# Thirteen expert jobs get their transposed tokens from VectorE and a DRAM exchange instead of from TensorE

## The chip, the cores and the metric

The kernel runs on one core of one Trainium2 chip. The metric is the time of the whole kernel on the device, in microseconds (us), as the median of several runs. The profile is that of one further execution.

## The reference, cut to what matters

The block takes 16 sequences of 256 tokens with 256 channels each: a normalisation with a shift, attention with 16 heads of width 64, a residual, and then a mixture of 8 experts. Every expert takes the 512 tokens that score highest for it (4096 tokens divided by 8), and adds its result to them, weighted by the gate:

```
gate = softmax(tok @ Wgate.T)
vals, idx = top_k(gate.T, 512)                  # for each expert
g = ln(tok[idx], mlp_g, mlp_b)
y = gelu(einsum('ked,ehd->keh', g, fc1s) + b1s) # 256 -> 1024
y = einsum('keh,edh->ked', y, fc2s) + b2s       # 1024 -> 256
tok = tok.at[idx].add(y * w)
```

All arithmetic of the large products is in float32.

## The kernel before

**Two parts.** The attention of all 16 sequences is laid out as a list of steps with written places (the long table `PLACES`); the steps are issued in that order. After it comes the loop over expert jobs, which the change touches. A job is one expert with one half of its tokens: there are two rounds of eight jobs. Jobs 0 to 7 take 256 tokens for each expert, chosen from the first 15 sequences; jobs 8 to 15 take 256 more for each, chosen from everything that is left. Jobs 0 and 1 are prepared inside the list of steps, and job 0's first matmuls too.

**One job.** `Job.load` (lines 1178 to 1186) brings the two weight matrices, 1 MB each, and the bias, on SP's DMA queue. `gives` and `onehot` (VectorE) make a table that says which token stands at which of the 256 places. `list_matmul` (line 1224, TensorE, 30 or 32 small matmuls) and `take` (lines 1233 and 1235, VectorE) turn it into two index columns and two weights. `gather` (line 1240) is two indirect DMAs from GpSimd (POOL) that fetch 128 normalised tokens of 1 KB each from `xn_dram` into `xg`. `transposes` (line 1249) turns the 256 tokens by 256 channels with four TensorE matmuls against the identity into PSUM tile `px`; `evict` (line 1256) copies it on ScalarE into `xT`, two instructions with the normalisation's gain and bias. Then come eight `up` steps (line 1268), each with a `gelu` (line 1275, ScalarE) after it, and eight `down` steps (line 1284), four for each half of the tokens. `finish` (line 1295, VectorE) weighs one half, and `scatter` (line 1301, POOL, an indirect DMA that adds) writes it to the output. The profile counts each float32 matmul of the source twice: an `up` or `down` step is four records, a job 64.

**The order of the work.** The loop runs k from 1 to 15. While job k computes, job k+1 (`new`) gets its list, its tokens and its transposes, and the one-hot table of job k+2 (`far`) is made. An iteration has 16 slots, one for each `up` or `down` step, and every engine receives its instructions in the order of the slots:

```
LIST_AT, TURN_AT, LATE_AT = 5, 14, 7
if new and s == (LATE_AT if late else LIST_AT):   # list_matmul, take, gather
if new and s == TURN_AT:                          # transposes, evict
```

Slots are an order of issue, not times: an engine goes ahead as far as its own data lets it, and all engines take their instructions strictly in this order. `lay_out(far)` starts one slot after `LIST_AT` and gives VectorE one piece (the table's head, then two or three one-hots) in each slot, through the end of the iteration and into the next one. At the end of iteration k, `far.load()` puts the weights of job k+2 on SP's queue; they go into the buffers of job k and so wait for its last `down`.

Iteration 7 is special (`late`): its `new`, job 8, is the first of the second round, so its whole one-hot table is made in slots 0 to 5 of that iteration and its list at slot 7. In iterations 1 to 6 the generator `second_routing` runs as well: at every fifth slot a small TensorE matmul (`count_three`, line 1049) and a group of VectorE instructions (`choose_bits`, `candidates`, `compare_three`, lines 1034 to 1064) search the second round's thresholds bit by bit.

**The exchange in the attention.** A way of transposing without TensorE is in use there already: VectorE turns blocks of 32 by 32 (lines 749 and 832, `STREAM_TRANSPOSE`), one DMA writes the turned blocks to a DRAM tile (lines 756 and 840), and four DMAs, one for each group of 32 partitions, read them back so that the blocks stand in exchanged places (lines 764 and 854).

Of the kernel before, what the change touches and what calls it, by code (L numbers as in the profile page):

```python
# [9 lines left out]
F32 = mybir.dt.float32  # L10
I32 = mybir.dt.int32
BF16 = mybir.dt.bfloat16
AF = mybir.ActivationFunctionType
# [5 lines left out]
P = 128  # L19
# [8 lines left out]
DC = D // P  # L28
# [3 lines left out]
KL = KC // 2  # L32
CAPL = CAP // 2
NV = 5
SQ = 32
QB = P // SQ
# [3 lines left out]
LN1_G, LN1_B, B_ADA, MLP_G, MLP_B = 0, 2, 4, 6, 8  # L40
# [4 lines left out]
class Plan:  # L45
# [7 lines left out]
    def step(self, place, engine, took, run, needs=(), makes=(), tiles=(), mode=0, lag=0.1):  # L53
        k = len(self.steps)
        self.steps.append((place, engine, took, run, needs, tiles, mode, lag))
        for m in makes:
            self.makers.setdefault(m, []).append(k)
# [7 lines left out]
def kernel(  # L65
# [14 lines left out]
    nc = tc.nc  # L80

    const = ctx.enter_context(tc.tile_pool(name="const", bufs=1))
    dram = ctx.enter_context(tc.tile_pool(name="dram", bufs=1, space=DRAM))
# [6 lines left out]
    vec = const.tile([P, NVEC], F32, name="vec")  # L90
# [432 lines left out]
    if True:  # L523
        attw = ctx.enter_context(tc.tile_pool(name="attw", bufs=1))
        seq = ctx.enter_context(tc.tile_pool(name="seq", bufs=2))
        work = ctx.enter_context(tc.tile_pool(name="work", bufs=2))
# [22 lines left out]
        class Shift:  # L549
            def __init__(self):  # L550
                self.pa = {}
# [75 lines left out]
        class First:  # L627
# [22 lines left out]
            def evict(self):  # L650
                b = self.b
                hTs[b] = seq.tile([P, DC, N], F32, tag="hT", name=f"hT{b}")
                for c in range(DC):
                    nc.scalar.activation(
                        hTs[b][:, c, :], self.pt[:, c, :], AF.Identity,
                        bias=bias1[:, c, b : b + 1],
                        scale=vec[:, LN1_G + c : LN1_G + c + 1],
                    )
# [12 lines left out]
        class Group:  # L671
# [74 lines left out]
            def turn(self, kb):  # L746
                if self.t == 0:
                    kb.append(work.tile([P, QB, TB, HP // 2, SQ], F32, tag="pb", bufs=3, name="kb"))
                nc.vector.transpose(
                    kb[0][:, :, self.t],  # L750
                    self.qk.rearrange("p (h q d) -> p q h d", q=QB, d=SQ),
                )

            def away(self, kb):
                self.blocks = dram.tile([QB, SQ, QB, N], F32, tag="blocks", bufs=4, name="kblocks")
                nc.sync.dma_start(
                    self.blocks.rearrange("k d q n -> (k d) (q n)"),
                    kb[0].rearrange("p q t h m -> p (q t h m)"),
                )

            def back(self):
                kT = self.keys()[:, self.g - 2].rearrange("p k t h m -> p k (t h m)")
                for q in range(QB):
                    nc.sync.dma_start(
                        kT[bass.ts(q, SQ)], self.blocks[:, :, q].rearrange("k d n -> d k n")
                    )

            def affine(self):
                kT = self.keys()[:, self.g - 2].rearrange("p k t h m -> p (k t h m)")
                nc.scalar.activation(  # L770
                    kT, kT, AF.Identity,
                    bias=vec[:, KN_B : KN_B + 1], scale=vec[:, KN_G : KN_G + 1],
                )
# [398 lines left out]
        class Job:  # L1172
            def __init__(self, e, routing, tiles):
                self.e, self.routing, self.tiles = e, routing, tiles
                self.oh = None

            def load(self):


                e = self.e  # L1180
                self.w2 = seq.tile([P, FC, D], F32, tag="oT", name="w2")
                nc.sync.dma_start(self.w2, fc2T[e].rearrange("(f p) d -> p f d", p=P))
                self.w1 = seq.tile([P, DC, DD], F32, tag="v", bufs=2, name="w1")
                nc.sync.dma_start(self.w1, fc1T[e].rearrange("(c p) f -> p c f", p=P))
                self.b2 = moe.tile([P, D], F32, tag="b2", bufs=2, name="b2")
                nc.sync.dma_start(self.b2, b2s[:, bass.ts(e, D)].to_broadcast([P, D]))
# [66 lines left out]
            def evict(self):  # L1253
                self.xT = seq.tile([P, DC, CAPL], F32, tag="hT", name="xT")
                for c in range(DC):
                    nc.scalar.activation(
                        self.xT[:, c, :], self.px[:, c, :], AF.Identity,
                        bias=vec[:, MLP_B + c : MLP_B + c + 1],
                        scale=vec[:, MLP_G + c : MLP_G + c + 1],
                    )  # L1260
                self.hid = seq.tile([P, FC, CAPL], F32, tag="qT", name="hid")
                self.y = work.tile([P, KL, D], F32, tag="pr", bufs=PRB, name="y")
                self.ph, self.py = {}, {}

            def up(self, f):
                self.ph[f] = ps.tile([P, CAPL], F32, tag="sc", bufs=4, name="ph")
                for c in range(DC):
                    nc.tensor.matmul(  # L1268
                        self.ph[f], self.w1[:, c, bass.ts(f, P)], self.xT[:, c, :],
                        start=(c == 0), stop=(c == DC - 1),  # L1270
                    )

            def gelu(self, f):
                k = B1 + self.e * FC + f
                nc.scalar.activation(  # L1275
                    self.hid[:, f, :], self.ph[f], AF.Gelu_apprx_tanh,
                    bias=vec[:, k : k + 1], scale=1.0,
                )

            def down(self, i, a=0, b=FC):  # L1280
# [51 lines left out]
        for b in range(B):  # L1332
# [16 lines left out]
            for (g, t), p in GROUP.items():  # L1349
                p += base  # L1350
                a = Group(b, g, t)
                n = (b, g, t)
# [23 lines left out]
            for d in range(HP // 2):  # L1376
                a = Quad(b, d)
                p = base + d * QUAD
                g = d // 2
                n = (b, d)  # L1380
                po = ("po", 0) + n
                for i in range(2):
                    q = p + 3 * i
                    m = n + (i,)
                    sums, pb, prT, blocks = ("sums",) + m, ("pb",) + m, ("prT",) + m, ("blocks",) + m
# [20 lines left out]
            for t in range(TB):  # L1406
                a = Tail(b, t)
                p = base + TAIL[t]
                n = (b, t)
# [55 lines left out]
        for n in range(2):  # L1465
            a = jobs[n]
            k = top + 10 + 20 * n
# [4 lines left out]
            for i in range(6):  # L1472
                name, took, by = {"D": ("DVE", 0.81, nc.vector), "P": ("POOL", 1.4, nc.gpsimd), "A": ("ACT", 3.5, nc.scalar)}[who[i]]
# [13 lines left out]
        k = top + 30  # L1487
# [9 lines left out]
        for k in plan.order(PLACES):  # L1497
            plan.steps[k][3]()

        LIST_AT, TURN_AT, LATE_AT = 5, 14, 7  # L1500
        SLOTS = 2 * FC

        def second_routing():
# [9 lines left out]
        def lay_out(job):  # L1513

            job.gives()
            for a in list(range(0, 18, 2)) + list(range(18, NT, 3)):
                yield
                job.onehot(a, a + (2 if a < 18 else 3))
# [5 lines left out]
        for k in range(1, len(jobs)):  # L1524
            a = jobs[k]
            new = jobs[k + 1] if k + 1 < len(jobs) else None
            far = jobs[k + 2] if k + 2 < len(jobs) else None
            late = k == last + 1
            for s in range(SLOTS):
                for step in next(rest, ()):  # L1530
                    step()
                if late and s == 0:
                    new.gives()
                if late and s < 6:
                    new.onehot(6 * s, 6 * s + 6)
                if new and s == (LATE_AT if late else LIST_AT):
                    for _ in () if late else parts:
                        pass
                    new.list_matmul(0, NT)
                    new.take()  # L1540
                    new.gather()
                    if k == 1:
                        jobs[0].scatter(by_end[1])
                if new and s == TURN_AT:
                    new.transposes()
                    new.evict()
                if not late and s < LIST_AT:
                    next(parts, None)
                if far and k != last and s > LIST_AT:
                    if s == LIST_AT + 1:  # L1550
                        parts = lay_out(far)
                    next(parts)
                if s < FC:
                    a.up(s)
                    a.gelu(s)
                    if s == FC - 1:
                        a.weigh()
                else:
                    i, q = divmod(s - FC, 4)
                    a.down(i, 2 * q, 2 * q + 2)  # L1560
                    if q == 3:
                        a.finish(i)
                        a.scatter(i)
            if far:
                far.load()
# [50 lines left out]
```

## Time and profile before

| | us |
|---|---|
| Runs shown | 1104.45, 1104.83, 1106.43 |
| Median | 1104.83 |
| The profiled execution, its time | 1106.04 |
| The profiled execution, its span (first to last instruction) | 1104.2 |

| Engine | busy us | share of the span |
|---|---|---|
| TensorE matmul (PE) | 1070.6 | 97% |
| VectorE (DVE) | 778.9 | 71% |
| GpSimd (POOL) | 616.2 | 56% |
| ScalarE (ACT) | 596.1 | 54% |

The granted clock of TensorE is 0.99 over the span. The expert loop begins at 865.6 us (first `up` of job 1) and its last matmul ends at about 1094.8 us. `SPq` names the instructions in SP's queue, almost all of them issues of DMAs. `px<-ident,xg` reads: written is `px`, read are `ident` and `xg`. `x4` means four instructions merged into one row. An entry in square brackets at the end of a row is the time for which the engine was idle before it, and what it waited for.

### The profile page before, as it was taken

Reading aid. Unit: us, or ns where it says so; the run is one execution under the profiler, and the core shown is the slowest. Engines: PE = TensorE matmul, PEld = TensorE weight load, DVE = VectorE, ACT = ScalarE, POOL = GpSimd, SP = SyncE. Lnnn points to the kernel's source line nnn. Section 1 sums busy time; section 2 is a strip of 40 time slices with the busy share of each in tenths; the row PEclk is TensorE's granted clock in tenths of the full one; section 3 lists DMA queues with packets and bytes.
Section 4 is the critical chain, followed back from the end, with each engine's and each line's share of the span. In section 5 each row is a group of like instructions: output and inputs, shape, how many; then the busy total and the mean of one; then the engine's idle time right before and its main releaser. Section 6 shows DMA issues by size and latency. Waiting matters only on the chain. (4 is left out here: it accounts for less than half of the span.)

```text
span 1104.2 us, 18872 instructions
## 1 busy us (share of the span) xinstructions
PE 1070.6 (97%) x5835; PEld 714.8 (65%) x5835; DVE 778.9 (71%) x2201; ACT 596.1 (54%) x1656; POOL 616.2 (56%) x997
## 2 busy tenths in 40 slices
PE   7999999999999999999899999999988999999996
PEld 4555656566565655656465655656767888888885
DVE  6657888777778777786678787676568488654540
ACT  2768666565766566566557667576522333322331
POOL 3766776776676665675657666565411233333332
PEclk9999999999999999999999999999999999999998
DMA  6013998785888787796787778895130456555661
GB/s 211 1 39 123 277 259 237 230 255 166 248 260 227 226 246 234 201 260 211 211 251 227 228 224 240 243 256 179 63 102 20 113 189 200 170 162 175 196 201 19
DMA packets 147539, 209.20 MB, mean 189 GB/s; under 512 B 15088, under 2 KB 122864, under 8 KB 147440
## 3 DMA queue, kind: packets, MB, share of 16 engines
q1 hardware_dynamic: 139520, 197.71, 60.0%
q0 software_dynamic: 6144, 8.39, 4.1%
q10 hardware_dynamic: 1776, 1.90, 0.5%
q8 instruction: 47, 0.77, 0.3%
q14 instruction: 52, 0.43, 0.1%
HBM read 121.96 MB, written 85.98 MB: 188 GB/s over the span
## 5 line engine op out<-in xcount | busy, mean ns | idle before, releaser
L683 PE MATMUL pm<-wq,hT 128*128 128x512 f32 x768 | 360.4, 605 | 5.0 <-DVE qk L716 2.8
L822 POOL TENSOR_SCALAR pr<-pr,sums 128x256 f32<-128x256 f32 x512 | 237.1, 481 | 112.2 <-DVE sums L818 92.9
L811 ACT ACTIVATE pr<-sc,nmax 128x256 f32<-128x256 f32 x512 | 238.0, 480 | 97.5 <-DVE nmax L802 80.3
L683 PEld LDWEIGHTS pm<-wq,hT 128*128 128x128 f32 x768 | 137.3, 192 | 146.1 <-issue 131.1
L103 POOL TENSOR_TENSOR ss<-ss,neghalf 128x8 f32<-128x8 f32 x128 | 210.5, 1645 | 10.6
L802 DVE TENSOR_REDUCE nmax<-sc 128x2 f32<-128x512 f32 x256 | 165.3, 676 | 16.9 <-PE sc L794 16.3
L832 DVE STREAM_TRANSPOSE pb<-pr 128x512 f32<-128x512 f32 x224 | 149.9, 690 | 18.5 <-POOL pr L822 13.6
L794 PE MATMUL sc<-kT,qT 64*128 64x256 f32 x1024 | 135.4, 397 | 0.0
L881 PE MATMUL po<-prT,v 128*64 128x256 f32 x1024 | 127.6, 388 | 1.1 <-DVE gates L950 1.1
L700 DVE TENSOR_REDUCE ss<-sq 128x8 f32<-128x512 f32 x128 | 86.0, 672 | 47.3 <-ACT sq L696 46.8
L794 PEld LDWEIGHTS sc<-kT,qT 64*128 64x128 f32 x1024 | 92.8, 188 | 40.8 <-issue 25.4
L696 ACT ACTIVATE sq<-pm 128x512 f32<-128x512 f32 x128 | 76.9, 603 | 77.3 <-PE pm L683 75.9
L1301 POOL DMA_INDIRECT out<-y,idx x32 | 51.2, 1601 | 119.8 <-DVE y L1295 66.9
L1268 PE MATMUL ph<-xT,w 128*128 128x256 f32 x512 | 117.6, 383 | 0.0
L907 PE MATMUL pw<-wo,oT 128*128 128x256 f32 x512 | 116.6, 381 | 0.3 <-DVE qk L716 0.3
L1284 PE MATMUL py<-w,hid 128*128 128x256 f32 x512 | 116.3, 380 | 0.0
L716 DVE TENSOR_TENSOR qk<-pm,ss 128x512 f32<-128x512 f32 x128 | 87.0, 681 | 36.9 <-POOL ss L103 35.9
L907 PEld LDWEIGHTS pw<-wo,oT 128*128 128x128 f32 x512 | 96.0, 190 | 23.2 <-issue 9.4
L811 ACT ACTIVATION_READ_ACCUMULATOR pr<-sc,nmax 128x1 f32 x512 | 107.6, 210 | 0.0
L881 PEld LDWEIGHTS po<-prT,v 128*64 128x64 f32 x1024 | 67.1, 137 | 61.5 <-issue 21.1
L1275 ACT ACTIVATE hid<-ph,vec 128x256 f32<-128x256 f32 x128 | 60.4, 474 | 84.2 <-PE ph L1268 76.3
L1284 PEld LDWEIGHTS py<-w,hid 128*128 128x128 f32 x512 | 95.6, 190 | 12.8
(140 smaller groups left out, 1132.6 us busy)
## 6 DMA issues: line engine op xcount, KB each, us to landing
blocks<-pb SPq DMA_DIRECT2D x112, 512.0 KB
prT<-blocks SPq DMA_DIRECT2D x448, 128.0 KB
w<-in_fc2T SPq DMA_DIRECT2D x16, 1024.0 KB
w<-in_fc1T SPq DMA_DIRECT2D x16, 1024.0 KB
kblocks<-kb SPq DMA_DIRECT2D x28, 512.0 KB
kT<-kblocks SPq DMA_DIRECT2D x112, 128.0 KB
out<-tok SPq DMA_DIRECT2D x32, 128.0 KB
xn_dram<-tn SPq DMA_DIRECT2D x32, 128.0 KB
```

What stands on the lines that cost most here:

```text
L103: nc.gpsimd.tensor_tensor(dst, src, neghalf[:, : src.shape[1]], ALU.pow)
L683: nc.tensor.matmul(self.pm, hTs[self.b][:, c, bass.ts(self.t, P)], wq[:, c, bass.ts(self.g, GW)], start=(c == 0), stop=(c == DC - 1),)
L716: engine.tensor_tensor(self.qk.rearrange("p (h d) -> p h d", d=HD), src.rearrange("p (h d) -> p h d", d=HD), self.ss[:, 1, :].unsqueeze(2) ...
L794: nc.tensor.matmul(self.sc[i, j][:, t, :], qTs[self.b][rows, hp, bass.ts(t, P)], keys[rows, hp] if direct else keys[rows, hp // 4, hp % 4] ...
L802: nc.vector.tensor_reduce(self.nmax[i, j], self.sc[i, j], AX.X, ALU.max, negate=True)
L811: nc.scalar.activation(self.pr[i, j][:, t, :], self.sc[i, j][:, t, :], AF.Exp, bias=self.nmax[i, j][:, t : t + 1], scale=1.0, accum_out=se ...
L822: nc.gpsimd.tensor_scalar(self.pr[i, j][:, t, :], self.pr[i, j][:, t, :], self.sums[i][:, 1, j, t : t + 1], 1.0, ALU.mult, ALU.mult,)
L832: nc.vector.transpose(self.pb[i][:, :, :, j].rearrange("p k c t n -> p t k c n"), self.pr[i, j].rearrange("p t (k c m) -> p t k c m", c=TB ...
L881: nc.tensor.matmul(self.po[j * HD : (j + 1) * HD, i, :], vs[self.b][:, c, bass.ts(4 * self.d + 2 * i + j, HD)], prT[:, j, c] if self.b in ...
L907: nc.tensor.matmul(self.pw, oTs[self.b][:, hp // 2, self.t, hp % 2, :], wo[:, hp, :], start=(hp == 0), stop=(hp == HP - 1),)
L1268: nc.tensor.matmul(self.ph[f], self.w1[:, c, bass.ts(f, P)], self.xT[:, c, :], start=(c == 0), stop=(c == DC - 1),)
L1284: nc.tensor.matmul(self.py[i], self.hid[:, f, bass.ts(i, P)], self.w2[:, f, :], start=(f == 0), stop=(f == FC - 1),)
```

## The change: what it does

For every `new` that is not `late`, which by the loop's bounds are jobs 2 to 7 and 9 to 15, thirteen in all, the four TensorE transposes and the eviction from PSUM are replaced by steps in four slots:

- slot 8, `turn`: two VectorE transposes of 32 by 32 blocks, each of 128 by 256 elements, from `xg` into a new tile `xb` (it uses buffers of the attention's `prT`);
- slot 9, `away`: one DMA on SP's queue, 256 KB, `xb` to the DRAM tile `xblocks`;
- slot 12, `back`: four DMAs on SP's queue, 64 KB each, from `xblocks` into `xT`; they wait for `away`'s landing;
- slot 15, `affine`: two ScalarE instructions of 128 by 256 that apply gain and bias to `xT` in place.

The tokens of `xT` then stand in another order (block of 32 first, half second). `up` reads its moving operand in pieces of 64 columns, and `gelu` writes its result back in the old order, in pieces of 32 columns; the rest of the job is as before. Jobs 0, 1 and 8 keep the old way.

The list step (`list_matmul`, `take`, `gather`) goes from slot 5 to slot 1, and with it the beginning of `lay_out(far)` from slot 6 to slot 2. In the first iteration the scatter of job 0's second half, which stands in the same step, moves along.

```
+            def turn(self):
+                self.xb = work.tile([P, QB, DC, KL, SQ], F32, tag="prT", bufs=4, name="xb")
+                for i in range(KL):
+                    nc.vector.transpose(
+                        self.xb[:, :, :, i].rearrange("p q c m -> p c q m"),
+                        self.xg[:, i].rearrange("p (c q d) -> p c q d", c=DC, d=SQ),
+                    )
+
+            def away(self):
+                self.blocks = dram.tile([QB, SQ, QB, P], F32, tag="xblocks", bufs=2, name="xblocks")
+                nc.sync.dma_start(
+                    self.blocks.rearrange("k d q n -> (k d) (q n)"),
+                    self.xb.rearrange("p q c i m -> p (q c i m)"),
+                )
+
+            def back(self):
+                self.xT = seq.tile([P, QB, DC, KL, SQ], F32, tag="hT", name="xT")
+                xT = self.xT.rearrange("p k c i m -> p k (c i m)")
+                for q in range(QB):
+                    nc.sync.dma_start(
+                        xT[bass.ts(q, SQ)], self.blocks[:, :, q].rearrange("k d n -> d k n")
+                    )
+
+            def affine(self):
+                for c in range(DC):
+                    xT = self.xT[:, :, c].rearrange("p k i m -> p k (i m)")
+                    nc.scalar.activation(
+                        xT, xT, AF.Identity,
+                        bias=vec[:, MLP_B + c : MLP_B + c + 1],
+                        scale=vec[:, MLP_G + c : MLP_G + c + 1],
+                    )
+                self.outputs()
...
-                        self.ph[f], self.w1[:, c, bass.ts(f, P)], self.xT[:, c, :],
+                        self.ph[f], self.w1[:, c, bass.ts(f, P)],
+                        self.xT[:, :, c].rearrange("p k i m -> p k (i m)") if self.exchanged else self.xT[:, c, :],
...
+                dst, src = self.hid[:, f, :], self.ph[f]
+                if self.exchanged:
+                    dst = dst.rearrange("p (i k m) -> p k i m", i=KL, m=SQ)
+                    src = src.rearrange("p (k i m) -> p k i m", i=KL, m=SQ)
...
-        LIST_AT, TURN_AT, LATE_AT = 5, 14, 7
+        LIST_AT, TURN_AT, LATE_AT = 1, 14, 7
+        EXCHANGE = {8: "turn", 9: "away", 12: "back", 15: "affine"}
...
-                if new and s == TURN_AT:
+                if new and late and s == TURN_AT:
                     new.transposes()
                     new.evict()
+                if new and not late and s in EXCHANGE:
+                    new.exchanged = True
+                    getattr(new, EXCHANGE[s])()
```

## The prediction

> **What bounds the kernel now.** I read the page's engine table first (PE 97% busy), then the PE timeline of the expert loop, because only that stage changes. Three rows around one set of transposes:
>
> ```profile
> 1043.19 5.34 PE L1284 MATMUL py<-w,hid 128*128 128x256 f32 x24
> 1048.37 0.60 PE L1249 MATMUL px<-ident,xg 128*128 128x128 f32 x4
> 1048.80 1.89 PE L1284 MATMUL py<-w,hid 128*128 128x256 f32 x8
> ```
>
> No row has an idle entry: PE sets the pace, and the four transposes take it from 1048.37 to 1048.80, 0.43 to 0.44 us. A job's first `up` stands at 1050.53, the next at 1065.67, then 1080.82: a job is 15.14 us (15.43 in iterations 1 to 6, 865.61 to 881.04). Whatever PE is spared is won, as long as the tokens are there in time. What they would wait for is in the other engines' rows. The timeline of one job that begins at 974.83 (my zero for such times, "t"; it is also when the last `down` of the job before ends):
>
> ```profile
> 971.90 1.62 POOL L1301 DMA_INDIRECT out<-y,idx  x1 [2.41 <-DVE y L1295]
> ...
> 975.02 0.37 SPq L1182 DMA_DIRECT2D w<-in_fc2T  x1
> 975.44 0.57 SPq L1184 DMA_DIRECT2D w<-in_fc1T  x1
> ...
> 976.54 1.62 POOL L1301 DMA_INDIRECT out<-y,idx  x1 [3.02 <-DVE oh L1216]
> ...
> 979.14 0.95 PE L1224 MATMUL pls<-give,oh 128*128 128x10 bf16 x32
> 980.13 0.16 DVE L1233 TENSOR_REDUCE idx<-pls 128x2 int32<-128x4 f32 x1 [2.25 <-PE pls L1224]
> 980.56 1.02 POOL L1240 DMA_INDIRECT xg<-xn_dram,idx  x1 [2.41 <-DVE idx L1233]
> 981.88 0.98 POOL L1240 DMA_INDIRECT xg<-xn_dram,idx  x1 [0.30 <-issue]
> ```
>
> The next job's weights (2 MB) are issued at t=0.2, the second scatter at t=1.7, the gathers at 5.7 and 7.05. The windows of the same job (PE, PEld, DVE, ACT, POOL, clock, DMA share, GB/s) show what they meet:
>
> ```profile
> 976.80:977.80 1.00, 1.00 (x6) 0.90 (x5) 1.00 (x7) 0.61 (x2) 1.00 (x1) 1.00 0.95 322
> ...
> 982.80:983.80 1.00, 1.00 (x6) 0.87 (x6) 0.45 (x4) 0.47 (x1) 0.06 (x1) 1.00 0.95 278
> 983.80:984.80 1.00, 1.00 (x7) 0.87 (x6) 0.00 (x0) 0.00 (x0) 0.00 (x0) 1.00 0.25 82
> 984.80:985.80 1.00, 1.00 (x6) 0.90 (x5) 0.00 (x0) 0.00 (x0) 0.00 (x0) 1.00 0.02 8
> ```
>
> The DMA engines are full from t=2 to t=9, then idle. For the new chain the nearest rows are a quiet exchange of the attention, on SP's queue, and the gathers' line in the tile view of `xg`:
>
> ```profile
> 68.99 0.34 SPq L756 DMA_DIRECT2D kblocks<-kb  x1
> 71.63 1.76 SPq L764 DMA_DIRECT2D kT<-kblocks  x4
> ```
>
> ```profile
> DMA to landing us min/median/max: 2.8/3.3/4.3
> ```
>
> **What it removes.** 13 x 0.44 = 5.7 us of PE. A job's PE work W becomes 14.70 us (14.99 in iterations 1 to 6).
>
> **The list, four slots earlier.** Its 32 matmuls, two reductions and two gathers all move. PE: two `up` records fewer stand before them, nothing is longer; the one-hots keep their 15 slots, and the last three (three at 0.17) run at t=0.7 to 1.2, before the list's last matmul at 1.8. In iteration 1 job 2's table is done at 856.6, long before. VectorE waits for the list at t=1.8, and behind it only one-hots queue. On POOL the gathers now follow the second scatter directly: it ends at t=3.33, the indices are there at 2.3, so the gathers are issued at 3.63 and 4.95 (the rows' 1.32 apart). The scatter of job 0 that moves along in iteration 1 goes behind the gathers, as now. In iteration 7, job 9's table head (0.65) and four one-hots (0.67) come ahead of job 8's last one-hot, which ends at 966.2 while its list begins at 965.7: about 1.0 us of PE wait, once (0 to 1.3).
>
> **The chain to the next job's first `up`**, from t=0:
> - *Tokens landed.* If a landing follows its issue: 4.95 + 3.3 = 8.25 (7.75 with the shortest). If the full DMA engines hold it, it stays at today's 7.05 + 3.3 = 10.35 (11.35 with the longest). The packet records speak for the second: the scatter issued at 976.54 moves its first packet at 981.3 (the one of 971.90 did at 974.0), and the gathers' packets follow it on the same queue from 983.0 on. I take 9.9, a little after the burst.
> - *Turn.* A 128x512 transpose takes 0.69; half the size between 0.34 and 0.69, I take 0.36 by size. VectorE has reached slot 8 by t=6 and stands waiting; the second transpose alone lies behind the landing. With the handover 0.6. The one-hots of slots 8 to 11 (1.35) and `finish` queue behind; `finish` may slip 0.8, and the scatter with it, which has 3 us to spare until the burst.
> - *Away.* 512 KB took 2.64 from issue to the first read-back; a 128 KB store lands in no less than 1.7. For 256 KB: 2.3.
> - *Back.* The four issues take 1.76, and the last of them landed 4.46 after the first issue by the trace's landings. Half the bytes, the same packets: 3.6 to 4.5, I take 4.2.
> - *Affine.* `xT`'s 0.56 today, 0.5 for the first of the two, and 0.3 to PE: 0.8. Behind it on ScalarE stand only the next job's `gelu`s, which need it anyway.
>
> Sum C = 9.9 + 0.6 + 2.3 + 4.2 + 0.8 = 17.8 us after t=0, where PE is free at 14.7. PE stalls 3.1 us (2.8 in iterations 1 to 6). The next weights' burst starts with the end of the last `down`, not with the delayed `up`, so the job after a stalled one has 3.1 us more and does not stall: the stalls come at every other job. Jobs 9, 11, 13, 15: 4 x 3.1 = 12.4; three of jobs 2 to 7: 3 x 2.8 = 8.4.
>
> **The clock after a gap.** A gap of 2.23 us in the attention was followed by half speed:
>
> ```profile
> 534.46 0.63 PE L725 MATMUL pq<-ident,qk 128*128 128x128 f32 x4 [2.23 <-DVE qk L716]
> ```
>
> ```profile
> 531.03:534.44 3.41, 1.19 (x12) 0.53 (x9) 2.50 (x6) 2.52 (x5) 3.07 (x5) 1.00 1.06 304
> 534.44:537.85 3.41, 3.39 (x20) 2.69 (x20) 2.19 (x4) 0.89 (x2) 3.00 (x5) 0.64 0.47 171
> ```
>
> The clock records have 3.41 us at 0.5 there, so such a gap costs up to 1.7 us more. With fixed windows a gap of 3 us fills most of one in some of the cases: 4 of 7, 6.8 us. The Trainium skill ("TensorE: Matmul & The Clock Gate", "What's actually happening") lets the clock fall after one idle window of about 3.4 us; by that none of these gaps would do it, and the sum would be 6.8 lower; the row above disagrees, and I go by the row.
>
> **At no cost.** VectorE's 26 transposes (9.4 us) lie beside its idle time (the windows' mean DVE share is 0.53); without that cover they would cost 0.7 per job. SP's 65 issues (13 x 2.1) find SP idle after the weights; the weights behind `back` are due at t=14.9 and `back` is issued by 14.3; if it were later, they have 5 us to spare in the job. The 0.5 MB per job fall into the idle DMA time after t=9. `up` with pieces in its moving operand: the attention's product reads `prT` in such pieces at the same 379 ns median. `gelu` with pieces in its output: `oT` is written in pieces in 587 ns against 592 for the plain copy of the same size; it would have to grow from 0.47 past the 0.86 of a slot to be seen.
>
> Sum: -5.7 + 1.0 + 12.4 + 8.4 + 6.8 = +22.9. Against the profiled execution 1106.0 + 22.9 = 1128.9; the median of the runs lies 1.2 lower: **1127.7**.
>
> **Rivals.**
> *The chain fits.* The gathers land as they are issued: 7.75 + 0.6 + 2.0 + 3.6 + 0.8 = 14.75, no stall, -5.7 and perhaps +1: **1100**. For it: nothing stands in POOL's way from 3.6 on, and iteration 1 has no scatter ahead. Against it: the late packets above. It decides below C = 15.6: there (C - W) / 2 equals the 0.44 won. The Trainium skill ("DMA: Bandwidth & Descriptors", "Queues, rings and completion order") lets each DMA engine take packets from its queues in turn; by that the gathers would not wait for the weights, C would be 16.1, and the sum about +5.
> *In between.* The landing moves up partly, C from 15.6 to 16.8, gaps too short for the clock: 4 x 1.5 + 3 x 1.2 - 4.7 = +4.9, about **1109**.
> *Worse.* VectorE, held by `turn`, delays the threshold search, whose groups (2.1 us) recur every five slots (4.3 us); PE then waits in `count_three` too; or C is 20 (11.35 + 0.6 + 2.7 + 4.5 + 0.9), 5.3 for each of seven stalls and the clock each time: **1148**.
>
> **How the numbers follow.** Forecast 0.66 (1112 to 1142), fits 0.12, in between 0.14, worse 0.08. A change within 0.2% (2.2 us) is about what the measurement cannot tell from none. Faster is all of the first rival and a little of the second, 0.14; same 0.05, from the second; slower 0.81. The ends of all terms together give 1100 and 1148; the range, 1106 to 1142, gives up the first rival and the worst, and holds the forecast and most of the second.
>
> **What would show it.** Right: twelve `px` records are left of 64; gathers issued near t=3.6 but landed near 10; SP's `back` waiting for `away`; idle PE before `ph` of every other job, ended by ACT `xT`, and rows with a clock below 1 after it. Wrong: `ph` rows without idle time, or landings three us after their issue.

## The result and the profile after

The changed kernel is slower, and by more than forecast.

| | before | after |
|---|---|---|
| Median of the runs, us | 1105.63 (1104.45 to 1106.68) | 1144.38 (1135.79 to 1146.28) |
| Ratio, 95% interval | | 1.0347 (1.0292 to 1.0402) |
| The profiled execution, its time | 1106.04 | 1135.79 |
| Its span | 1104.2 | 1133.9 |
| Expert loop, first `up` of job 1 to the end of the last `down` | 229.2 | 261.1 |

The forecast was 1127.7, in a range that ended at 1142. A fifth run on record took 1148.97. The profiled execution happens to be the fastest of these runs; a later trace of the same kernel, below, shows a slower one (1147.37).

The page gives the sum of what went wrong in one group and one row. The group is the `up` matmuls (busy time, mean ns of one, then the idle time ahead of them and what ended it); the row is the granted clock in 40 slices of the span. Before:

```profile
PEclk9999999999999999999999999999999999999998
...
L1268 PE MATMUL ph<-xT,w 128*128 128x256 f32 x512 | 117.6, 383 | 0.0
```

After:

```profile
PEclk9999999999999999999999999999989898999999
...
L1305 PE MATMUL ph<-xT,w 128*128 128x256 f32 x512 | 130.2, 411 | 24.1 <-ACT xT L1290 24.1
```

Before, that group had no idle time. Now TensorE stands 24.1 us in front of `up`, all of it ended by the gain and bias on ScalarE, the last step of the new chain; and the mean `up` record has grown from 383 to 411 ns, because the clock falls in several slices of the loop. The timeline of TensorE shows where (start, duration, and in brackets the idle time before the row):

```profile
879.71 1.19 PE L1305 MATMUL ph<-xT,w 128*128 128x256 f32 x4 [1.27 <-ACT xT L1290]
897.63 2.08 PE L1305 MATMUL ph<-xT,w 128*128 128x256 f32 x4 [2.60 <-ACT xT L1290]
...
1004.30 1.19 PE L1305 MATMUL ph<-xT,w 128*128 128x256 f32 x4 [2.53 <-ACT xT L1290]
...
1020.86 1.03 PE L1305 MATMUL ph<-xT,w 128*128 128x256 f32 x4
...
1040.06 1.71 PE L1305 MATMUL ph<-xT,w 128*128 128x256 f32 x4 [4.34 <-ACT xT L1290]
```

In the second round every other job stalls: jobs 9, 11, 13 and 15 by 2.53, 4.34, 4.02 and 2.75 us, and jobs 10, 12 and 14 not at all (1020.86 has no entry). In the first round all of jobs 2 to 7 stall: 1.27, 2.60, 1.33, 2.92, 1.22 and 1.08. One whole chain, that of job 11, is in the timeline of all engines; t=0 is 1020.86, where job 10 begins:

```profile
1021.05 0.40 SPq L1183 DMA_DIRECT2D w<-in_fc2T  x1
...
1023.11 1.58 POOL L1342 DMA_INDIRECT out<-y,idx  x1 [3.12 <-DVE idx L1234]
1024.99 1.53 POOL L1241 DMA_INDIRECT xg<-xn_dram,idx  x1 [0.30 <-DVE oh L1217]
1026.83 0.98 POOL L1241 DMA_INDIRECT xg<-xn_dram,idx  x1 [0.30 <-issue]
...
1032.02 0.90 DVE L1267 STREAM_TRANSPOSE xb<-xg 128x256 f32<-128x256 f32 x2 [6.39 <-DMA xg<-xn_dram,idx]
1032.95 0.34 SPq L1274 DMA_DIRECT2D xblocks<-xb  x1
1035.02 1.75 SPq L1283 DMA_DIRECT2D xT<-xblocks  x4
1039.41 1.09 ACT L1290 ACTIVATE xT<-xT,vec 128x256 f32<-128x256 f32 x2 [10.08 <-DMA xT<-xblocks]
```

Gathers issued at t=4.1 and 6.0, VectorE idle until the first has landed at t=11.2 (the second at 11.6), away at 12.1, back at 14.2, gain and bias at 18.6, `up` at 19.2. TensorE was free 4.34 us earlier.

The clock follows the gaps. Windows around the stall before job 13 (length, busy us of PE, PEld, DVE, ACT and POOL with instruction counts, clock, DMA share, GB/s):

```profile
1071.00:1074.60 3.60, 0.06 (x1) 0.00 (x0) 1.43 (x9) 0.17 (x1) 0.64 (x1) 1.00 0.72 142
1074.60:1078.00 3.40, 2.92 (x37) 2.38 (x38) 0.00 (x0) 1.40 (x3) 1.58 (x1) 0.50 0.98 324
1078.00:1081.40 3.40, 3.40 (x8) 2.69 (x9) 2.96 (x16) 0.47 (x1) 2.38 (x2) 0.50 1.02 329
```

One idle stretch, and then two windows of 3.41 us at half speed. In the loop the clock records hold eight such windows, 27.3 us, each costing half its length: 13.7 us. The parts of the loop's +31.9 us are then -5.7 (transposes gone) + 24.1 (idle) + 13.7 (clock) = 32.1. The loop happened to begin 2.3 us earlier in this execution, which leaves the span's +29.7.

### The profile page after: what moved, and what is told of

Its sections match the earlier page's. It is cut to its first block, busy times and chain, and to the rows that moved or that the text cites. A ratio compares the mean times of both kernels' runs of the same rounds, so it can differ in the third digit from the quotient of the medians.

```text
span 1133.9 us, 18898 instructions
## 1 busy us (share of the span) xinstructions
PE 1078.0 (95%) x5783; PEld 715.3 (63%) x5783; DVE 785.4 (69%) x2227; ACT 596.9 (53%) x1656; POOL 620.1 (55%) x997
## 5 line engine op out<-in xcount | busy, mean ns | idle before, releaser
L802 DVE TENSOR_REDUCE nmax<-sc 128x2 f32<-128x512 f32 x256 | 165.3, 676 | 16.4 <-PE sc L794 15.8
L1305 PE MATMUL ph<-xT,w 128*128 128x256 f32 x512 | 130.2, 411 | 24.1 <-ACT xT L1290 24.1
L1305 PEld LDWEIGHTS ph<-xT,w 128*128 128x128 f32 x512 | 101.2, 204 | 43.8 <-ACT xT L1290 29.3
```

The lines of the kernel that those rows point to most:

```text
L802: nc.vector.tensor_reduce(self.nmax[i, j], self.sc[i, j], AX.X, ALU.max, negate=True)
L1305: nc.tensor.matmul(self.ph[f], self.w1[:, c, bass.ts(f, P)], self.xT[:, :, c].rearrange("p k i m -> p k (i m)") if self.exchanged else sel ...
```

## The experiments

The theory: TensorE waits for a chain whose head, the landing of the gathers, is held by the burst of the next weights; what the list's earlier place gives is therefore small; the gaps bring the clock down. The rivals: the exchange and the list's place cost each by itself (what the early list moves on the queues), or the chain's own DMAs and VectorE's order are what delays it. The first trace added a question, why *all* jobs of the first round stall.

### One part alone: the list in slot 1, TensorE still transposing

```diff
-                if new and late and s == TURN_AT:
+                if new and s == TURN_AT:
                     new.transposes()
                     new.evict()
-                if new and not late and s in EXCHANGE:
+                if False:
```

> Only the list step moves from slot 5 to slot 1; the transposes stay on TensorE in slot 14. Theory (the loss lies in the chain from the gathers to the next job's first up): the four transposes are done in slot 14 whatever the list's slot, so no ph row has idle time in front, and the time is that of before, 1105.6, give or take 1.5; the gathers are issued near t=3.6 and land between 8 and 10.5. Rival (the list's move itself costs, because its matmuls then wait for one-hots or its gathers meet the weights): idle time in front of pls or px, and a time above 1110.

Measured: 1105.07 against 1105.15, ratio 0.9999 (0.9986 to 1.0012). No time in front of `up`. The tile view of `xg`, the line of the gathers:

```profile
DMA to landing us min/median/max: 2.8/5.7/7.2
```

Before, the line read 2.8/3.3/4.3. The gathers are issued some 2 us earlier and take 2.4 us longer: in the median their landing has not moved forward (the landings that the trace has lie at t=9.4 to 11.7, later than the expected 8 to 10.5; job 8, with its later list, is left out). Moving the list costs nothing by itself.

### The other part alone: the exchange, the list back in slot 5

```diff
-        LIST_AT, TURN_AT, LATE_AT = 1, 14, 7
+        LIST_AT, TURN_AT, LATE_AT = 5, 14, 7
```

> Only the exchange; the list stays in slot 5. Theory (the landing of the gathers is held by the full DMA engines, near t=10 in a job without a stall): in jobs that did not stall the gathers, issued at 5.7 and 7.05, land at 10 to 11.4 as before the change, and the next first up comes 17.5 to 19.5 after t=0 as with the change. In a job that did stall the list itself comes 2.7 to 4 us later, the gathers are issued at 8.5 to 11 and land at 12.5 to 14, so the job after it stalls too, by 1 to 3 us; seven such cases put the time some 7 to 20 above the changed kernel's 1136 to 1146, at 1145 to 1165. Rival (the landing follows the issue): in every job the chain is 2 us longer than with the change, the first case included: next first up at 19.4 to 21 after t=0 in unstalled jobs.

Measured: 1153.96, ratio 1.0454 (1.0437 to 1.0472). The page's group:

```profile
L1305 PE MATMUL ph<-xT,w 128*128 128x256 f32 x512 | 133.1, 418 | 34.1 <-ACT xT L1290 34.1
```

The whole loss comes with the exchange: +48.8 us alone, and +38.8 with the early list. In the iteration of job 8 the gathers land at t=10.9 and 11.3 and the next `up` comes at 19.6; with the early list it came at 17.4 in that iteration (18.9 in the second trace, below). In the iteration of job 1, the other one without a stall at its start, it comes at 18.3 instead of 16.4 (16.7). The landing is where the theory had it (10 to 11.4), but the chains are 0.7 to 2.2 us longer, near the 2 us of the rival, so this run does not separate the two. The early list is worth about 10 us, but only to a kernel that has the late chain.

### The suspected cause: no weights arrive during the loop

Jobs 2 to 15 keep the weights and biases of jobs 0 and 1, so the 2 MB per job are left out, and the products are those of other experts.

```diff
-        jobs[2].load()
+        jobs[2].w1, jobs[2].w2, jobs[2].b2 = jobs[0].w1, jobs[0].w2, jobs[0].b2
...
-                far.load()
+                far.w1, far.w2, far.b2 = a.w1, a.w2, a.b2
```

> The changed kernel, but jobs 2 to 15 use the weights and the bias of the second matrices of jobs 0 and 1 again instead of loading their own, so the 2 MB at the start of each job are left out (the result is that of other weights). Theory (the weights' transfer holds the gathers): the gathers, issued near 3.6 and 4.95, land 2.5 to 3.3 later, at 7.5 to 8.3; with turn 0.9, write 2.1, read-back 3.5 to 4, gain and bias and handover 0.8 the next first up is ready at 15 to 16, stalls of at most 1.3 at every other job, no half clock after them: 1101 to 1109. Rival (the chain is long by its own latencies and the scatter ahead of the gathers, not by the weights): landings still near 10, time above 1125.

Measured: 1113.95, ratio 1.0095 (1.0077 to 1.0113): 30 us of the 39 are gone, and the time is 5 us above the range that the theory gave. The landing line of `xg`, and the chain of a job that begins at 1008.25, in the timeline:

```profile
DMA to landing us min/median/max: 2.7/2.8/4.4
```

```profile
1012.33 1.02 POOL L1241 DMA_INDIRECT xg<-xn_dram,idx  x1 [0.30 <-DVE oh L1217]
1013.65 0.97 POOL L1241 DMA_INDIRECT xg<-xn_dram,idx  x1 [0.30 <-issue]
...
1016.52 0.45 DVE L1267 STREAM_TRANSPOSE xb<-xg 128x256 f32<-128x256 f32 x1 [0.90 <-DMA xg<-xn_dram,idx]
1016.99 0.34 SPq L1274 DMA_DIRECT2D xblocks<-xb  x1
...
1019.14 1.73 SPq L1283 DMA_DIRECT2D xT<-xblocks  x4
...
1023.25 1.19 PE L1305 MATMUL ph<-xT,w 128*128 128x256 f32 x4
```

Without the burst the gathers land 2.8 us after their issue, and the chain ends at t=15.0 instead of 17.4 to 19.2: most second-round jobs then start at 14.8 to 16.0. Two outliers remain, at 17.4 and 18.9. The rest of the loss stands in the first round (1.51, 2.67, 1.29, 0.70 and 0.21 us in front of jobs 2 to 6). In two of its iterations the tokens had landed by t=8.2 and 10.6, but VectorE, behind its threshold search, turned them only at 11.9 and 12.4. That is a delay that my sum had not held.

### The clock: TensorE kept busy in the gap

```diff
+            if new and not late:
+                fill(12)
             if far:
                 far.load()
```

`fill(12)` is twelve idle transposes, 1.3 us, issued after the last `down`.

> The changed kernel with 12 idle TensorE transposes (1.3 us, nobody reads them) between the last down of a job and the first up of the next, where the next one's tokens come by the exchange. Theory (a stall is a wait for a fixed point of time, and half of the loss behind a stall is the clock that falls after the gap): the fills lie inside the waits; two successive jobs lose 3.1 to 4.5 in total as before, split more evenly, and the half-clock windows in the loop (eight after the profiled change) fall to three or fewer: 7 to 12 us faster than the changed kernel, 1126 to 1136. Rival (fills add to TensorE's work): 13 x 1.3 = 17 us more, above 1153.

Measured: 1131.90 (1130.83 to 1137.99), ratio 1.0250 (1.0233 to 1.0268), 12.5 us below the changed kernel. The page's clock row:

```profile
PEclk8999999999999999999999999999999999999999
```

Two windows at half speed are left in the loop, of eight to ten; they stand behind gaps of 4.92 and 3.14 us. Six to eight windows fewer are 10 to 14 us. The time without useful work did not shrink: in this trace (the slowest of the runs, 1137.99) TensorE is idle for 14.2 us ahead of `up`, and the thirteen fills take 17 more, against 24.1 and, in the second trace below, 32.9 us of idle time in the changed kernel. So the gain is the clock's.

### The first round: the second scatter behind the gathers

All six jobs of the first round stall in the changed kernel. Its POOL timeline shows how (in each group the scatters of a job's first and second half, then the first of the next gathers):

```profile
914.61 1.62 POOL L1342 DMA_INDIRECT out<-y,idx  x1 [10.13 <-DVE oh L1217]
921.68 1.56 POOL L1342 DMA_INDIRECT out<-y,idx  x1 [5.45 <-DMA out<-y,idx]
923.55 1.02 POOL L1241 DMA_INDIRECT xg<-xn_dram,idx  x1 [0.31 <-DVE three L1034]
...
932.08 1.61 POOL L1342 DMA_INDIRECT out<-y,idx  x1 [6.23 <-DVE oh L1217]
941.68 1.58 POOL L1342 DMA_INDIRECT out<-y,idx  x1 [7.98 <-DMA out<-y,idx]
943.56 1.02 POOL L1241 DMA_INDIRECT xg<-xn_dram,idx  x1 [0.30 <-DVE three L1034]
```

The second scatter adds to the same output and waits for the first one's landing. Before, the two of a job were issued 4.6 to 4.7 us apart, the first 1.6 to 3.0 us ahead of the job's end in this round; here they are 7.1 and 9.6 apart. The first comes late (932.08 is the end of the last `down`), because VectorE's `finish` queued behind `turn`; it runs into the weights' burst, holds the second up, and the gathers stand behind that on POOL. Late tokens make a late `turn`, and that makes the next late scatter: a loop. The VectorE timeline, somewhat earlier, has the start of the first of these:

```profile
906.76 0.16 DVE L1055 TENSOR_SCALAR_CACHE_REDUCE enough<-pc 128x3 f32<-128x3 f32 x1 [3.28 <-PE pc L1049]
...
909.93 0.76 DVE L1267 STREAM_TRANSPOSE xb<-xg 128x256 f32<-128x256 f32 x2
...
913.86 0.48 DVE L1336 SCALAR_TENSOR_TENSOR y<-py,w,bw 128x256 f32<-128x256 f32 x1
```

The tokens had landed by 906.6. VectorE waited for a count of the search, did its group, turned at 909.93 and came to `finish` at 913.86. To break the loop, the second scatter is issued after the next list's gathers:

```diff
                     new.gather()
-                    if k == 1:
-                        jobs[0].scatter(by_end[1])
+                    if not late:
+                        jobs[k - 1].scatter(1)
...
                         a.finish(i)
-                        a.scatter(i)
+                        if i == 0 or k in (last, len(jobs) - 2, len(jobs) - 1):
+                            a.scatter(i)
```

> The changed kernel, but the scatter of a job's second half is issued after the next list's gathers instead of ahead of them. Theory (a loop: VectorE waits in turn, so finish of the first half and its scatter come late and fall into the next weights' transfer; the second scatter waits for the first one's landing, and the gathers queue behind it on POOL): the gathers are issued 2.2 us after their job's first up in every job, land between 8 and 12 after t=0 and never at 14 to 16, the next first up comes at most 20 after t=0; the time falls to 1122 to 1136. Rival (the scatters don't matter, only the weights and the search on VectorE): landings and time as with the change, 1136 to 1148.

Measured: 1120.42 (1118.10 to 1122.98), ratio 1.0135 (1.0119 to 1.0150): 24 us below the changed kernel, and 1.6 under the expected range. POOL in the iteration of job 4, whose t=0 is 918.4:

```profile
922.34 1.01 POOL L1241 DMA_INDIRECT xg<-xn_dram,idx  x1 [3.10 <-DVE idx L1234]
923.65 0.98 POOL L1241 DMA_INDIRECT xg<-xn_dram,idx  x1 [0.30 <-issue]
924.94 1.62 POOL L1342 DMA_INDIRECT out<-y,idx  x1 [0.30 <-issue]
```

The gathers are issued at t=3.9 and 5.2, and by the packet records the last of their packets ends at t=9.5; over all exchanged jobs it ends at 8.4 to 11.0. One iteration is not as expected: in iteration 3 the gathers are issued only at t=7.3 and 8.6, `turn` begins at 15.2, and the next `up` comes at 22.2 instead of 20 at most. 14.2 us of idle time are left, in pieces of 0.5 to 2.6 us, with three half-speed windows (10.2 us): -5.7 + 14.2 + 5.1 = 13.6 of the loop's +16.4; 2.8 us of it are in none of these rows. The idle time is 7.0 us in the first round (10.4 and, in the second trace below, 16.9 in the changed kernel) and 7.2 in the second (13.6 and 16.0). So the order on POOL is worth these 24 us, and the burst holds the gathers even when nothing stands ahead of them on POOL. The second round, whose scatters were not late in this way, gains as much as the first: there the last gather packet ends at t=8.4 to 10.2, against 9.6 to 12.7 in the changed kernel's first trace. The edit breaks the loop and also gives the gathers an earlier place on POOL's queue; which share of the gain is the loop's was not measured.

### The second round alone, and the changed kernel once more

```diff
-                if new and late and s == TURN_AT:
+                if new and k <= last + 1 and s == TURN_AT:
...
-                if new and not late and s in EXCHANGE:
+                if new and k > last + 1 and s in EXCHANGE:
```

> The exchange for jobs 9 to 15 only; jobs 2 to 7 keep TensorE's transposes, the list is in slot 1 for all. Theory (each round loses for itself): the profiled change lost 2.7, 4.5, 4.2 and 2.9 us in front of jobs 9, 11, 13 and 15, some 14, with four half-clock windows worth up to 6.8, less 7 x 0.44 = 3.1: 12 to 18 us above before, 1117 to 1124. If the threshold search of the first round were the main cause: below 1112.

Measured: 1123.19, ratio 1.0169 (1.0153 to 1.0184), and stalls at every other job only, each ended by ScalarE's `xT` (two of them, in the TensorE timeline):

```profile
990.75 2.08 PE L1305 MATMUL ph<-xT,w 128*128 128x256 f32 x4 [4.12 <-ACT xT L1290]
...
1061.95 2.08 PE L1305 MATMUL ph<-xT,w 128*128 128x256 f32 x4 [5.35 <-ACT xT L1290]
```

The others are 2.86 and 2.52. Seven exchanged jobs: -3.1 + 14.9 (idle) + 8.5 (five half-speed windows) = +20.3, measured +18.9. About half of the loss belongs to this round.

A second trace of the changed kernel, with no edit:

> The changed kernel once more, for a second trace: its first profiled execution took 1135.8 us, its other runs 1143 to 1149. If the loop through the scatters sets the spread, a slower execution shows more jobs whose first scatter is issued after the last down of its job and lands 6 us or more later, and gathers landing at 14 or later behind them; if the clock sets it, more half-clock windows than the eight of the first profile.

Measured: 1144.89 (1142.41 to 1147.37), ratio 1.0363 (1.0339 to 1.0387). Its page has

```profile
L1305 PE MATMUL ph<-xT,w 128*128 128x256 f32 x512 | 131.7, 414 | 32.9 <-ACT xT L1290 32.9
```

and in job 5 the same late scatter (POOL timeline; the job begins at 931.2):

```profile
931.47 1.61 POOL L1342 DMA_INDIRECT out<-y,idx  x1 [6.24 <-DVE oh L1217]
941.24 1.58 POOL L1342 DMA_INDIRECT out<-y,idx  x1 [8.16 <-DVE cand L1064]
```

Idle time of 1.52, 2.59, 1.35, 2.94, 1.85 and 6.68 us before jobs 2 to 7, and of 4.03, 3.99, 3.95 and 3.99 before jobs 9, 11, 13 and 15; ten half-speed windows. -5.7 + 32.9 + 17.1 = 44.3, and the loop is 43.1 longer than before. The two traced executions, 11.6 us apart, differ in the stalls (8.8 us more) and in the clock (3.4 us more), and gathers land at t=14 or later in three iterations of the slower one, in one of the other. For the other runs this is not shown.

### What starts the loop: the turn ahead of the search

The search's group stood ahead of `turn` in iteration 3. Here `turn` goes ahead of it, to slot 6 in iteration 2 and slot 5 in iteration 3:

```diff
+                slots = {**EXCHANGE, **{8: None, 8 - k: "turn"}} if k in (2, 3) else EXCHANGE
-                if new and not late and s in EXCHANGE:
+                if new and not late and slots.get(s):
                     new.exchanged = True
-                    getattr(new, EXCHANGE[s])()
+                    getattr(new, slots[s])()
```

> The changed kernel, but in iterations 2 and 3 VectorE's turn is issued in slots 6 and 5, ahead of the group of the threshold search that stood in front of it (in iteration 3 the turn began at 15.1 and 13.6 us after t=0 in the two traces, with the tokens landed at 11.8 and 11.3). Theory (turn waits behind the search there, finish and the first scatter behind turn, and this scatter is the first to fall into the next weights' transfer): iteration 3's turn begins within 0.6 of the second landing, its first scatter is issued before the job's last down and lands in 4 us, the stalls in front of jobs 4 to 7, 7.2 and 13.5 us in the two traces, fall below 7, the time to 1130 to 1140. Rival (the lateness comes from the gathers alone): the turn moves and scatters of later jobs still fall into the transfer, 1141 to 1148.

Measured: 1146.53 (1141.71 to 1148.55), ratio 1.0379 (1.0362 to 1.0397): no gain, and my theory said there would be one. The VectorE timeline:

```profile
908.20 0.45 DVE L1267 STREAM_TRANSPOSE xb<-xg 128x256 f32<-128x256 f32 x1 [4.87 <-DMA xg<-xn_dram,idx]
...
909.64 0.15 DVE L1055 TENSOR_SCALAR_CACHE_REDUCE enough<-pc 128x3 f32<-128x3 f32 x1
...
916.07 0.48 DVE L1336 SCALAR_TENSOR_TENSOR y<-py,w,bw 128x256 f32<-128x256 f32 x1
```

`turn` now follows the landing at once, but VectorE idles 4.87 us for it, and the search's groups come between `turn` and `finish`, which is as late as before; the scatter behind it is issued at 916.83, 1.2 us ahead of the weights, and the second one only 5.7 us after it. TensorE now waits for the search as well (its timeline):

```profile
911.75 0.16 PE L1049 MATMUL pc<-cnt,block 128*128 128x3 bf16 x1 [3.04 <-DVE reach L1042]
```

This is the wait in `count_three` that the prediction's rival *Worse* named; the changed kernel itself has none in the first trace and 0.66 us in the second. The stalls before jobs 4 to 7 are 8.7 us, where the theory had less than 7. So exchanging the two does not cure it: VectorE has too much queued behind one late landing, whichever comes first. Which of these delays is the first in iterations 2 to 4 stays open.

### A version with a whole job of slack

If the landing cannot move, the chain can get time. Here the list is made *two* iterations ahead (slot 6), `turn` and `away` stand in slot 12 of that iteration, when the burst is over, and `back` and the gain and bias in slots 1 and 13 of the next. The exchange serves jobs 3 to 7 and 11 to 15; jobs 2, 8, 9 and 10 keep TensorE's transposes, and job 3's table is made ahead of the loop. The core of the diff:

```diff
+        ahead = set(range(3, 8)) | set(range(11, 16))
...
+                if s == 6 and k + 2 in ahead:
+                    listed(far)
...
+                if k + 1 in ahead and s == 1:
+                    new.back()
+                if k + 1 in ahead and s == 13:
+                    new.affine()
+                if k + 2 in ahead and s == 12:
+                    far.turn()
+                    far.away()
```

`listed` is `list_matmul`, `take` and `gather`; the table of job k+3 is begun in slot 7.

> The exchange with a whole job of slack: for jobs 3 to 7 and 11 to 15 the list is made in slot 6 of the iteration two before their own, turn and away in slot 12 of it, behind finish of the first half, the read-back in slot 1 and gain and bias in slot 13 of the iteration after; jobs 2, 8, 9 and 10 keep TensorE's transposes; job 3's one-hots are made before the loop. Theory (only the missing slack made the exchange lose): no idle time in front of any ph row, ten times 0.44 us won: 1101.2, between 1099.5 and 1103.5. Rival (the extra 0.5 MB per job or the turns hold something else up, the scatters, the weights or the threshold search): idle time in front of ph, pc or pls and a time above 1104.5.

Measured: 1101.28 (1099.85 to 1103.43) against 1104.32, ratio 0.9973 (0.9964 to 0.9982): 3.0 us faster than the kernel before, and faster than the changed one. The page's group, TensorE's timeline (two jobs) and, from the timeline of all engines, one chain:

```profile
L1305 PE MATMUL ph<-xT,w 128*128 128x256 f32 x512 | 117.7, 383 | 0.0
```

```profile
1020.22 5.34 PE L1305 MATMUL ph<-xT,w 128*128 128x256 f32 x24
...
1034.92 5.34 PE L1305 MATMUL ph<-xT,w 128*128 128x256 f32 x24
```

```profile
1017.37 0.76 DVE L1267 STREAM_TRANSPOSE xb<-xg 128x256 f32<-128x256 f32 x2
1018.16 0.34 SPq L1274 DMA_DIRECT2D xblocks<-xb  x1
...
1022.06 2.32 SPq L1283 DMA_DIRECT2D xT<-xblocks  x4
...
1031.25 1.09 ACT L1290 ACTIVATE xT<-xT,vec 128x256 f32<-128x256 f32 x2 [2.56 <-DMA xT<-xblocks]
```

Jobs 10 to 13 take 14.70 us each, as the prediction's W, the PE work of a job, said. No `up` row has an idle entry (two rows of the list, in iterations 5 and 9, have 0.2 and 0.3 us), and no window of the loop runs at half speed. `xT` is ready at 1032.3, 2.6 us before its job. Ten jobs at 0.44 us would be 4.4 us, of which 3.0 (2.0 to 4.0 by the interval) arrive in the median.

## Why the prediction was right or wrong

**Right: the sign and the mechanism.** PE set the pace and lost it to a chain of DMAs; four transposes at 0.44 us are 5.7 us, and the kernel with slack has the job of 14.70 us that the text worked out. The early list is free and worthless by itself (ratio 0.9999); job 8's 1.0 us of wait did not show (no idle entry at its list).

**Right: the landing is held by the burst.** The rival that the gathers land as issued gave C = 14.75; with the burst taken away most jobs start at 14.8 to 16.0, with it the unstalled ones brought the next at 17.4 to 19.2. By the packet records it is the start that is held. With the list alone in slot 1 the second scatter's first packet moves 4.9 to 5.0 us after its issue, without the weights 2.2; the gathers' packets follow behind it, and the gathers land at a median of 5.7 us after issue, without the weights 2.8. With the gathers issued ahead of the scatter their own first packet comes mostly 3.6 to 4.4 us after issue, without the weights about 1.7. So part of the gathers' wait was the scatter ahead of them, which the burst had held. The Trainium skill ("DMA: Bandwidth & Descriptors", "Queues, rings and completion order") lets a DMA engine take packets from its queues in turn. The packet records do not speak against that: in 2.5 us around the end of one burst (kernel with the gathers ahead of the scatter, 990.5 to 993.0) 201 packets of POOL's queue stand beside 238 of SP's. But the estimate that the gathers would therefore not wait did not hold, because of the late start; why it is late is not shown.

**Right: the terms behind the landing.** In the four unstalled jobs 8, 10, 12 and 14 `turn` to `away` took 0.5 (0.6 in the sum), `away` to the first read-back 2.1 (2.3), back 3.9 to 4.3 (4.2), the affine to `up` 0.76 (0.8). The two transposes are 0.45 us each against the estimate of 0.36.

**A size off: the landing, 9.9.** In these jobs it was 10.1 to 11.6, mean 10.8; the stalls of jobs 9, 11, 13 and 15 average 3.4 against 3.1 (4.0 in the second trace). My bounds, 8.25 and 11.35, held the mean, and two of the four (11.4 and 11.6) lie above the upper one. I put the term too close to the burst's end at 9.

**A size off: the clock, 6.8.** It is 13.7 us in this trace and 17.1 in the second. Five of the six gaps of 2.5 to 4.4 us were followed by half speed, and three of these five by two windows instead of one: the term had one window at most per gap and 4 of 7 gaps. The Trainium skill ("TensorE: Matmul & The Clock Gate", "What's actually happening") lets the clock fall after an idle window of about 3.4 us; by that most of these gaps would cost nothing, and gaps of 2.53 and 2.60 us with half speed behind them disagree. Going by the attention's row was right.

**Wrong: "`finish` may slip 0.8, and the scatter with it, which has 3 us to spare until the burst", and with it "three of jobs 2 to 7".** The 3 us are read from a job of the second round (971.90 against 974.83). In the first round, where VectorE searches too, the first scatter of job 3 had only 1.6 us before the change (POOL timeline; job 4 begins at 911.92), and that of job 4 had 2.2:

```profile
910.32 1.62 POOL L1301 DMA_INDIRECT out<-y,idx  x1 [5.76 <-DVE y L1295]
```

After it, job 3's scatter slipped by the 0.8 allowed, to 1.0 us ahead of the weights (914.61, weights at 915.58), and took 6.3 us to land instead of 3.9. The second scatter waited for that landing, and the next gathers behind it on POOL; the scatters of jobs 4 and 5 then slipped by 2.3 and 1.9 us (2.5 each in the second trace). In the second round scatters issued 0.7 and 0.9 us ahead of their job's end still landed in 4.1 and 4.0 us: SP was issuing `back` until t=15.9, not 14.3 as the prediction had it, and the weights came 1.1 to 1.3 us after the end. Instead of a stall at every other job of the first round there were six, 10.4 us here and 16.9 in the second trace, against 8.4; that 10.4 is near 8.4 is luck: six stalls of 1.7 us on average stand there instead of three of 2.8. The rival *Worse* named the search, but as a wait of PE in `count_three`, and not this loop through POOL. The kernel with the second scatter behind the gathers recovers 24 us, in both rounds, so the order on POOL, which the sum had at nothing, is worth more than any of its terms. Why VectorE is late in the first place in iterations 2 to 4 is open.

**The sum.** Stalls +3.3, clock +6.9, the list of job 8 -1.0, an earlier start of the loop -2.3 and rounding: that is the step from the forecast +22.9 to the measured +29.7 in the profiled execution. The second trace has 8.8 us more idle and 3.4 us more from the clock.

## What to carry to other kernels

Before an operation is moved off the engine that sets the pace, add up the whole latency of what takes its place, with its head at the time when the data really land (here behind the 2 MB of the next weights), and compare it with the period; 0.44 us won per job is not worth a 3 us stall. Here the chain paid with a whole period of slack and lost without; anything between was not tried. Where an instruction waits for data from a queue, list what stands behind it on the same engine and follow it to the next gather: a late wait may come back as a later one.

## What the runs showed of the hardware that was not expected

- One gap can cost two half-speed windows. The stall of 2.60 us before job 3 was followed by 6.83 us at clock 0.50, that of 2.53 before job 9 by 3.41, and that of 2.75 before job 15 by none; gaps of 1.1 to 1.3 us were never followed by any. The length alone does not decide: over the traces of all experiments gaps in front of `up` of 1.80, 1.81 and 1.85 us were followed by a half-speed window, others of 2.50 to 2.75 us were not.
- Gathers issued during the burst landed near its end: those issued at t=4.1 and 6.0 by t=11.6; issued ahead of the scatter, at t=3.9 and 5.2, their last packet ended at t=9.5, and issued at 2.3 and 3.6, the earliest here, at 8.4. Without the burst they take 2.8 us.
- Twelve idle transposes, 1.3 us in all, at each handover left two of eight to ten half-speed windows and won 12.5 us. The two stood behind remaining gaps of 3.14 and 4.92 us.
